# When a batch's weights and rows enter the DMA queue: ring weights by halves in six slots, rows of x behind a slot's swaps, the first output rows a slot sooner

## The chip, the core and the metric

The kernel runs on one core of a Trainium2 chip, in float32 throughout. The metric is the device time of one execution in microseconds, lower is better. TensorE (PE in the profile) multiplies, VectorE (DVE), ScalarE (ACT) and GpSimd (POOL) do the rest, and SyncE (SP) issues nearly all transfers, one after the other, in the order in which the program writes them down.

## The reference

Cross-attention of a sequence to a context that serves as keys and values, with a layernorm before and a residual after. There are 8 batches of 256 rows, 256 context rows and 1024 columns, 32 heads of 32.

```python
x = (hidden - mu) * rsqrt(var + 1e-5) * ln_gamma + ln_beta
Q = split_heads(x @ Wq.T)          # K = V = split_heads(ctx)
scores = einsum('bhsd,bhtd->bhst', Q, K) * 32 ** -0.5
probs  = softmax(where(mask, scores, -inf))
attn   = einsum('bhst,bhtd->bhsd', probs, V)
out    = hidden + attn.reshape(B, S, 1024) @ Wout.T
```

## The kernel before

**Slots.** The work of a batch is cut into 8 slots of 4 heads each, so there are 64 slots, numbered n = 8 b + i. The order of all instructions is written out by hand in one loop over n. In slot n, PE computes the scores of slot n + 1 (L494), the products of probabilities and values of slot n - 2 (L645), and pieces of the two projections (L216). DVE, ACT and POOL do the softmax of slot n + 1.

**Queries seven products at a time.** From batch 2 on, Q = xn Wq is made by a Strassen-like scheme of seven smaller products, one in a slot, the first in slot first = 8 (b - 1) + 2 (`firsts`, L817): S1, S4, A11, S2, S3, A22, A12. Each has 64 matmuls, 16 for each of four blocks of columns. Three of them take their weights from one buffer of 1 MB called `ring`: S1 uses T1, A11 (slot first + 2) uses B11, and S3 (slot first + 4) uses T3. T1, B11 and T3 are made once in the first batches and kept in DRAM (`kept`, L405 to L411). For batches 3 to 7 they are fetched into the ring each time by `load_ring(name, half)` (L417, L419), 512 KB a half; half 0 holds the first two blocks, so the first 32 matmuls of a product, half 1 the last 32. A half can only be overwritten when the product before has read it.

**Swaps.** The transposed probabilities of a slot go through four small transfers on SP: a first pair pT<-pT (L623), which waits for ACT's copies (`aside`, L564) and DVE's transposes (L558), and a second pair pT<-pc (L627), which overwrites what the first pair reads and so waits until it has landed. The end of `softmax_parts` writes down, in this order: the loads in the list `ahead`, the first pair, the loads in the list `between`, the second pair.

```python
for r in range(2):
    nc.sync.dma_start(pT[ts(2 * r, K), 1], pT[ts(2 * r + 1, K), 0])
for load in between:
    load()
for r in range(2):
    nc.sync.dma_start(pT[ts(2 * r + 1, K), 0], pc[ts(2 * r, K)])
```

In slots below 8 and above 55 this tail runs inside the next slot's softmax, while the `ahead` loads stay where they are.

**Other transfers.** Each slot loads keys (L135, 256 KB for two slots) or values (L143, 512 KB for two slots) in `between`. `load_x` (L129) brings the rows of a later batch for its layernorm, 512 KB for each half of the rows; DVE takes their statistics (L234) and transposes them (L323), then 16 moves of 64 KB each (`move_x`, L339) stand behind the swaps of slots first - 6 to first - 4 (4, 6 and 6 of them). `load_res` (L149) brings rows of x for the residual, 256 KB in four pieces a batch, to which POOL adds one product (L762) and DVE the others (L771) before they are stored (L772).

**Where the loads stand before the change.** T1's halves in `between` of slots first - 3 and first - 2; both halves of B11 in `ahead` of slot first; both halves of T3 in `ahead` of slot first + 2. Rows of x in `between` of slots first - 13 and first - 12 (first - 12 and first - 11 for batch 3). The first output rows in `between` of the batch's slot i = 0.

Of the kernel before, what the change touches and what calls it, by code (L numbers as in the profile page):

```python
# [59 lines left out]
def xattn_kernel(  # L60
# [11 lines left out]
    B, S, D = x.shape  # L72
# [3 lines left out]
    NQ = NC  # L76
# [9 lines left out]
    N = B * NQ  # L86
# [75 lines left out]
    B11, B21, B22, T1, T2, T3, T4 = range(7)  # L162
# [222 lines left out]
    SPLIT = 2  # L385
# [423 lines left out]
    for n in range(N):  # L809
# [7 lines left out]
    firsts = {NQ * (b - 1) + 2: b for b in range(SPLIT, B)}  # L817
# [1 line left out]
    assert not any(n in products and new_qs[n] for n in range(N))  # L819


    loads, stats, norms, trans, moves, biases, masks = (
        {n: [] for n in range(N)} for _ in range(7)
    )
    for b in range(1, B):
        first = NQ * (b - 1) + 2
        if b == 1:
            when = dict(moves=())
        elif b == 2:
            when = dict(  # L830
                loads=(0, 1), stats=(2, 3), norms=(3, 4), trans=(4, 5),
                moves=tuple(5 + (i + 2) // 6 for i in range(16)),
            )
        else:
            when = dict(
                loads=(first - 12, first - 11) if b == SPLIT + 1 else (first - 13, first - 12),
                stats=(first - 10, first - 8) if b == SPLIT + 1 else (first - 11, first - 9),
                norms=(first - 8, first - 7), trans=(first - 7, first - 6),
                moves=tuple(first - 6 + (i + 2) // 6 for i in range(16)),
            )  # L840
        for table, key in (
            (loads, "loads"), (stats, "stats"), (norms, "norms"), (trans, "trans"),
        ):
            for i, n in enumerate(when.get(key, ())):
                assert n < first
                table[n].append((b, i))
        for n in range(N):
            part = [i for i, slot in enumerate(when["moves"]) if slot == n]
            if part:
                assert n < first - 1  # L850
                moves[n].append((b, part))
        biases[NQ * b - 2].append(b)
        if b % 2 == 0:
            masks[NQ * b - 7].append(b)
# [18 lines left out]
    S3_SLOTS = [(b, NQ * b + {0: NQ, 1: NQ - 1}.get(b, NQ - 2)) for b in range(B)]  # L873


    away, rings = {n: [] for n in range(N)}, {n: [] for n in range(N)}
    for n, name, half in (
        (8, "T1", 0), (8, "T1", 1), (9, "B11", 0), (10, "B11", 1), (13, "T3", 0), (14, "T3", 1),
    ):
        away[n].append(partial(keep_wq, name, half))  # L880
    for n, b in firsts.items():
        for slots, name in (((n - 3, n - 2), "T1"), ((n, n), "B11"), ((n + 2, n + 2), "T3")):
            if b > SPLIT:
                for half, slot in enumerate(slots):
                    rings[slot].append(partial(load_ring, name, half))


    ln_stats(0, 0)
# [17 lines left out]
    for c in range(NC):  # L906
        copy_x0(1, c, nc.scalar if c < NC // 2 else nc.vector)
    first = softmax_parts(0, (partial(copy_q, 1), partial(copy_q, 2)), (), (), {}, [
        partial(ln_stats, 1, 0), partial(ln_stats, 1, 1),
        partial(ln_norm, 1, 0, nc.vector),  # L910
    ])
# [16 lines left out]
    for b in range(B - 1):  # L928
        done, ends = 0, b == B - 2
        for i, counts in enumerate(steps_of(b)):  # L930
            n = NQ * (b + 1) + i
# [15 lines left out]
    for n in range(N):  # L947
        b, i = divmod(n - NQ, NQ)
        new_q = new_qs[n]
        between = []  # L950
        if n % 2 and n + 1 < N:
            between.append(partial(load_v, n + 1))
        elif n % 2 == 0 and n + 4 < N:
            between.append(partial(load_k, n + 4))
        ahead = rings[n]
        if n + 3 in firsts or n + 2 in firsts:
            between, ahead = between + ahead, []
        if b >= 0:
            if b == B - 2 and i - 1 in (5, 6):
                between.append(partial(send, b, *ENDS_TO[i - 1]))  # L960
            if i < 4:
                between.append(partial(load_res, b, *((0, 0), (0, 1), (1, 1), (1, 0))[i]))
        between += [partial(load_x, *args) for args in loads[n]]
        between += [partial(load_mask, one) for one in masks[n]]
        if n in (2, 4):
            between.append(partial(load_wo, B21, n // 2 - 1))
# [205 lines left out]
```

## Time and profile before

| | us |
|---|---|
| median of 3 runs | 565.37 (564.01 to 566.51) |
| the profiled execution, whole | 565.4 |
| its span, first to last instruction | 563.6 |
| PE busy in the span | 556.2 |
| DVE, ACT, POOL busy | 467.4, 423.4, 394.8 |

PE's clock is granted in full through the whole span. The DMA engines move 119.43 MB, 212 GB/s on average. Times in the profile count from the span's start. A matmul's start is measured and its end is modelled. In the tables of waits a row names the waiting engine and line, what it waited for, and then the total, the number of times and the longest. "SPq" is SP's queue as it issues; the duration of an issue is not that of the transfer.

### The profile page before, as it was taken

The numbers are of one execution on the slowest core, as the hardware profiler recorded it, in microseconds if no ns is written. First come the engines' busy times: TensorE is split into PE (matmuls) and PEld (weight loads), VectorE is DVE, ScalarE is ACT, GpSimd is POOL, SyncE is SP. The second block draws the span as 40 slices with busy tenths as digits, with TensorE's granted clock in tenths as the row PEclk, the third lists the DMA queues.
The fourth block names the chain that finished last, engine by engine and source line by source line (L and its number), as shares of the span: only waits on it lengthen the run. The fifth ranks groups of instructions, "written<-read, shape, count | busy, mean of one in ns | idle before, by whom it ended". The sixth has DMA issues, their size and how long they took to land.

```text
span 563.6 us, 26534 instructions
## 1 busy us (share of the span) xinstructions
PE 556.2 (99%) x10364; PEld 350.8 (62%) x10364; DVE 467.4 (83%) x1716; ACT 423.4 (75%) x1464; POOL 394.8 (70%) x636
## 2 busy tenths in 40 slices
PE   8999999999999999999999999998999999999997
PEld 8666664666656667566765676566765767644443
DVE  5979889999997988888898888986878878879923
ACT  3699998898768867787777977777767776869920
POOL 2688887899786675876569665776658657448780
PEclk9999999999999999999999999999999999999999
DMA  8967657966798767887779668786667874536751
GB/s 302 396 187 208 168 158 213 305 199 168 226 299 248 217 181 197 259 249 222 196 223 283 204 185 232 237 263 174 166 168 251 260 207 135 153 101 184 208 170 74
DMA packets 47244, 119.43 MB, mean 212 GB/s; under 512 B 8976, under 2 KB 9744, under 8 KB 47120
## 3 DMA queue, kind: packets, MB, share of 16 engines
q1 hardware_dynamic: 46976, 117.74, 69.8%
q8 instruction: 82, 1.34, 1.0%
q14 instruction: 42, 0.34, 0.2%
q10 hardware_dynamic: 144, 0.01, 0.0%
HBM read 66.33 MB, written 11.53 MB: 138 GB/s over the span
## 4 chain that ended last, share of the span: by engine, by line
PE 77%; DVE 6%; POOL 6%; DMA 5%; SPq 2%; issue 2%; ACT 2%; DVEq 0%; POOLq 0%
PE po_S L216 17%; PE pq_A L216 16%; PE pv L645 10%; PE sc L494 9%; PE po_A L216 8%; PE pq L216 6%; PE pq_S L216 6%; PE po_end L216 3%; DVE pT L558 2%; DMA pT<-pT 2%; DMA r<-in_x_dram 2%; ACT e L537 1%; POOL e L552 1%; DVE e L533 1%; PE po_last L216 1%
## 5 line engine op out<-in xcount | busy, mean ns | idle before, releaser
L552 POOL TENSOR_SCALAR e<-e,rden 128x256 f32<-128x256 f32 x466 | 215.4, 479 | 119.8 <-DVE rden L544 116.9
L537 ACT ACTIVATE e<-e,mn 128x256 f32<-128x256 f32 x512 | 254.1, 502 | 41.7 <-DVE mn L533 41.3
L558 DVE STREAM_TRANSPOSE pT<-e 128x512 f32<-128x512 f32 x256 | 179.0, 704 | 35.6 <-POOL e L552 26.9
L533 DVE CUSTOM_DVE_ANT_0 e<-sc,mb 128x256 f32<-128x256 f32 x512 | 185.3, 416 | 22.0 <-PE sc L494 21.4
L564 ACT COPY pc<-pT 128x512 f32<-128x512 f32 x128 | 78.9, 617 | 54.7 <-DVE pT L558 35.2
L537 ACT ACTIVATION_READ_ACCUMULATOR e<-e,mn 128x1 f32 x512 | 98.2, 192 | 0.0
L645 PE MATMUL pv<-pT,v 64*32 64x128 f32 x4096 | 74.4, 274 | 0.4 <-DMA pT<-pc 0.4
L216 PE MATMUL po_S<-wo,at 128*64 128x512 f32 x304 | 73.9, 599 | 0.0
L645 PEld LDWEIGHTS pv<-pT,v 64*32 64x32 f32 x4096 | 57.0, 105 | 26.6 <-ACT pc L564 10.8
L494 PE MATMUL sc<-k,qa 32*64 32x256 f32 x2048 | 72.1, 387 | 0.2 <-ACT qa L301 0.2
L494 PEld LDWEIGHTS sc<-k,qa 32*64 32x64 f32 x2048 | 37.6, 131 | 49.2 <-issue 33.0
L216 PE MATMUL po_A<-wo,at 128*64 128x512 f32 x256 | 58.6, 599 | 0.0
L216 PE MATMUL pq<-xnT,wq 128*64 128x256 f32 (+3 forms) x544 | 58.4, 369 | 0.0
L216 PEld LDWEIGHTS pq_A<-xnT,wq 128*64 128x64 f32 x832 | 46.6, 137 | 7.1 <-issue 5.7
L216 PE MATMUL po_S<-wo,s 128*64 128x512 f32 x208 | 49.8, 600 | 0.7 <-DVE r L771 0.7
L216 PEld LDWEIGHTS pq<-xnT,wq 128*64 128x64 f32 x544 | 36.8, 136 | 19.1 <-issue 1.7
L216 PE MATMUL pq_A<-xnT,wq 128*64 128x128 f32 x832 | 47.8, 273 | 0.0
L544 DVE RECIPROCAL rden<-den 128x2 f32<-128x2 f32 x256 | 38.3, 150 | 7.3 <-ACT e L537 6.2
L533 DVE DVE_READ_ACCUMULATOR2_ANT mn<- 128x1 f32 x512 | 42.6, 83 | 0.0
L216 PEld LDWEIGHTS po_A<-wo,at 128*64 128x64 f32 x256 | 16.9, 136 | 30.0 <-issue 28.7
L762 POOL TENSOR_TENSOR r<-r,p 128x512 f32<-128x512 f32 x24 | 30.8, 1282 | 6.8 <-DMA r<-in_x_dram 4.4
L216 PEld LDWEIGHTS po_S<-wo,at 128*64 128x64 f32 x304 | 20.3, 136 | 21.9 <-issue 21.6
(100 smaller groups left out, 646.1 us busy)
## 6 DMA issues: line engine op xcount, KB each, us to landing
v<-in_kv_dram SPq DMA_DIRECT2D x32, 512.0 KB, 4.8
pT<-pT SPq DMA_DIRECT2D x128, 128.0 KB, 3.2
pT<-pc SPq DMA_DIRECT2D x128, 128.0 KB, 4.1
ring<-kept_T SPq DMA_DIRECT2D x20, 512.0 KB
k<-in_kv_dram SPq DMA_DIRECT2D x32, 256.0 KB, 3.8
x<-in_x_dram SPq DMA_DIRECT2D x15, 512.0 KB, 5.6
r<-in_x_dram SPq DMA_DIRECT2D x28, 256.0 KB, 4.5
out_dram<-r SPq DMA_DIRECT2D x28, 256.0 KB, 2.6
```

The costliest lines, as they stand in the source:

```text
L216: nc.tensor.matmul(out[ts(w, P // 2)], stationary[:, ts(w, P // 2)], moving, **flags)
L494: nc.tensor.matmul(scs[n][j][ts(w, P // 2), s, :], qa[r, n % NQ, ds(s * P + w * P // 2, P // 2)], ks[n - n % 2][r, n % 2, :], start=True, ...
L533: nc.vector.tensor_tensor_reduce(out=e[:, s, :], in0=pss[j][:, s, :], in1=mbs[n // NQ], scale=1.0, scalar=NO_SCORE, op0=ALU.add, op1=ALU.m ...
L537: nc.scalar.activation(e[:, s, :], e[:, s, :], AF.Exp, bias=mn[:, s : s + 1], scale=-1.0, accum_out=den[:, s : s + 1],)
L544: nc.vector.reciprocal(rden, dens[j])
L552: engine.tensor_scalar(es[j][:, s, :], es[j][:, s, :], rden[:, s : s + 1], 1.0, ALU.mult, ALU.mult,)
L558: nc.vector.transpose(pT[:, :, :, j, :, :].rearrange("p a i s k -> p (a i) s k"), es[j].rearrange("p s (b t) -> p b s t", t=K),)
L564: nc.scalar.copy(pc[:, :, ts(j, 2)], pT[:, 1, :, ts(j, 2)])
L645: nc.tensor.matmul(pvs[n][r][j * HD : (j + 1) * HD], vs[n - n % 2][ts(r, 2 * K), i, ds(n % 2 * P + j * HD, HD)], pT[ts(r, 2 * K), :, i, j, ...
L762: nc.gpsimd.tensor_tensor(r, r, p1s[b], ALU.add)
```

## The change

The ring halves no longer go out in pairs. For batches 3 to 7:

| load | before | after |
|---|---|---|
| T1, half 0 | `between` of slot first - 3 | `ahead` of slot first - 2 |
| T1, half 1 | `between` of slot first - 2 | `ahead` of slot first - 1 |
| B11, half 0 | `ahead` of slot first | `between` of slot first |
| B11, half 1 | `ahead` of slot first | `ahead` of slot first + 1 |
| T3, half 0 | `ahead` of slot first + 2 | `between` of slot first + 2 |
| T3, half 1 | `ahead` of slot first + 2 | `ahead` of slot first + 3 |

Rows of x for batches 3 to 7 move from `between` of a slot to `ahead` of the next, which is behind the second pair of swaps of the old slot and in front of the first pair of the new one. The first output rows of a batch (`load_res(b, 0, 0)`) go from slot i = 0 to `between` of slot i = 7 before it. The amount of data and all work of the engines stay the same.

```diff
             when = dict(
-                loads=(first - 12, first - 11) if b == SPLIT + 1 else (first - 13, first - 12),
+                early_loads=(first - 11, first - 10) if b == SPLIT + 1 else (first - 12, first - 11),
...
-        for slots, name in (((n - 3, n - 2), "T1"), ((n, n), "B11"), ((n + 2, n + 2), "T3")):
+        for slot, name in ((n - 2, "T1"), (n, "B11"), (n + 2, "T3")):
             if b > SPLIT:
-                for half, slot in enumerate(slots):
-                    rings[slot].append(partial(load_ring, name, half))
+                (rings if name == "T1" else rings_between)[slot].append(partial(load_ring, name, 0))
+                rings[slot + 1].append(partial(load_ring, name, 1))
...
-        ahead = rings[n]
-        if n + 3 in firsts or n + 2 in firsts:
-            between, ahead = between + ahead, []
+        ahead = [partial(load_x, *args) for args in early_loads[n]] + rings[n]
+        if i == NQ - 1 and b + 1 < B - 1:
+            between.append(partial(load_res, b + 1, 0, 0))
         if b >= 0:
             if b == B - 2 and i - 1 in (5, 6):
                 between.append(partial(send, b, *ENDS_TO[i - 1]))
-            if i < 4:
-                between.append(partial(load_res, b, *((0, 0), (0, 1), (1, 1), (1, 0))[i]))
-        between += [partial(load_x, *args) for args in loads[n]]
+            if 0 < i < 4:
+                between.append(partial(load_res, b, *((0, 1), (1, 1), (1, 0))[i - 1]))
+        between += rings_between[n] + [partial(load_x, *args) for args in loads[n]]
```

More of the change, by code (lines that the diff above doesn't have):

```diff
@@ L819, in xattn_kernel @@
     assert not any(n in products and new_qs[n] for n in range(N))
-    loads, stats, norms, trans, moves, biases, masks = (
-        {n: [] for n in range(N)} for _ in range(7)
+    loads, stats, norms, trans, moves, biases, masks, early_loads = (
+        {n: [] for n in range(N)} for _ in range(8)
     )
@@ L841, in xattn_kernel @@
         for table, key in (
-            (loads, "loads"), (stats, "stats"), (norms, "norms"), (trans, "trans"),
+            (loads, "loads"), (early_loads, "early_loads"), (stats, "stats"), (norms, "norms"), (trans, "trans"),
         ):
@@ L873, in xattn_kernel @@
     S3_SLOTS = [(b, NQ * b + {0: NQ, 1: NQ - 1}.get(b, NQ - 2)) for b in range(B)]
-    away, rings = {n: [] for n in range(N)}, {n: [] for n in range(N)}
+    away, rings, rings_between = ({n: [] for n in range(N)} for _ in range(3))
     for n, name, half in (
```

## The prediction

> **What bounds the kernel now.** I read the page's busy shares first, then the waits of TensorE, then those of the DMA queue, then the queue in order of time. The page:
>
> ```profile
> span 563.6 us, 26534 instructions
> ...
> PE 556.2 (99%) x10364; PEld 350.8 (62%) x10364; DVE 467.4 (83%) x1716; ACT 423.4 (75%) x1464; POOL 394.8 (70%) x636
> ...
> PE 77%; DVE 6%; POOL 6%; DMA 5%; SPq 2%; issue 2%; ACT 2%; DVEq 0%; POOLq 0%
> ```
>
> TensorE (PE) is busy for 556.2 of 563.6 us. The chain of waits runs through DVE, POOL and DMA for a fifth of the span, which looks like room; the waits say how much there is. First PE's own waits, then one of the queue's (total, times, longest):
>
> ```profile
> PE pq_S L216 <- issue: 1.7, 1, 1.7
> ...
> PE po_S L216 <- DVE r L771: 0.7, 1, 0.7
> PE pv L645 <- DMA pT<-pc: 0.4, 1, 0.4
> ```
>
> ```profile
> SPq L627 <- DMA pT<-pT: 63.3, 49, 5.5
> ```
>
> Inside the work PE lacks a result only twice, for 0.7 and 0.4 us; the 1.7 us of "issue" have no cause that the profile names. So a transfer that comes sooner can win about 1 us, at most about 3, while one that comes too late stops the engine that sets the end. The question is lateness. The queue itself waits 63.3 us at L627: the second pair of swaps (pT<-pc) overwrites what the first pair (pT<-pT, L623) reads, so SP stands still until the first pair has landed, and everything behind stands with it. Here is the queue through slots 23 and 24 (start, duration):
>
> ```profile
> 221.88 0.53 SPq L772 DMA_DIRECT2D out_dram<-r  x1
> 222.51 1.15 SPq L623 DMA_DIRECT2D pT<-pT  x2
> 223.71 0.57 SPq L143 DMA_DIRECT2D v<-in_kv_dram  x1
> 224.33 0.45 SPq L419 DMA_DIRECT2D ring<-kept_T  x1
> 224.87 1.15 SPq L627 DMA_DIRECT2D pT<-pc  x2
> 226.11 0.54 SPq L772 DMA_DIRECT2D out_dram<-r  x1
> 227.00 2.18 SPq L623 DMA_DIRECT2D pT<-pT  x2
> ...
> 229.85 0.45 SPq L419 DMA_DIRECT2D ring<-kept_T  x1
> 230.42 1.40 SPq L149 DMA_DIRECT2D r<-in_x_dram  x1
> 233.57 1.15 SPq L627 DMA_DIRECT2D pT<-pc  x2
> ```
>
> Two things are to be seen. From first to second pair takes 2.36 us (222.51 to 224.87) with no large load in front, and 6.57 us (227.00 to 233.57) behind v, a ring half, a pair of swaps and a store. And T1's second half goes out at 229.85, inside that wait; it doesn't stand behind it.
>
> **The change, part by part.** *T1, second half.* It moves from between the swaps of slot first-2 to the front of slot first-1. In the queue that is behind the second pair: past the 3.7 us wait just shown and the pair's own 1.15 us. S1, the first product of a batch, needs it for its second 32 of 64 matmuls. The chain in order of time gives S1 of batches 4 to 7, S3 of batch 4 and the stop of 1.7 us (start, us):
>
> ```profile
> 236.27 3.49 PE pq_S L216 x64
> ...
> 269.75 3.65 PE pq_A L216 x64
> ...
> 303.42 3.49 PE pq_S L216 x64
> ...
> 370.20 3.50 PE pq_S L216 x64
> ...
> 382.03 1.69 issue
> ...
> 438.99 3.49 PE pq_S L216 x64
> ```
>
> Batch 3's S1 stands in PE's timeline, where the 0.7 us wait follows it:
>
> ```profile
> 168.38 3.66 PE L216 MATMUL pq_S<-sx,ring 128*64 128x128 f32 x64
> 172.76 1.94 PE L216 MATMUL po_S<-wo,s 128*64 128x512 f32 x8 [0.72 <-DVE r L771]
> ```
>
> The second half is needed 1.75 us after S1 starts (half of 3.49). Issue today in batches 3, 5, 6 and 7 (batch 4's is 229.85 above):
>
> ```profile
> 164.24 0.44 SPq L419 DMA_DIRECT2D ring<-kept_T  x1
> ```
>
> ```profile
> 296.90 0.54 SPq L419 DMA_DIRECT2D ring<-kept_T  x1
> ```
>
> ```profile
> 362.74 0.45 SPq L419 DMA_DIRECT2D ring<-kept_T  x1
> ```
>
> ```profile
> 431.40 0.45 SPq L419 DMA_DIRECT2D ring<-kept_T  x1
> ```
>
> How long 512 KB takes to land, and how fast the DMA engines move data in a full stretch:
>
> ```profile
> v<-in_kv_dram SPq DMA_DIRECT2D x32, 512.0 KB, 4.8
> ...
> ring<-kept_B SPq DMA_DIRECT2D x10, 512.0 KB, 7.5
> ...
> kept_T<-ring SPq DMA_DIRECT2D x4, 512.0 KB, 3.3
> ```
>
> ```profile
> 290.00:300.00 10.00, 10.00 (x162) 5.14 (x156) 8.69 (x31) 7.26 (x26) 9.06 (x17) 1.00 0.98 297
> ```
>
> The page has no landing for ring<-kept_T. I take v's 4.8 us: same size, one load at a time; B11's 7.5 is for two halves back to back, the store's 3.3 is the short end. A load of 512 KB (524 kB) in front of a swap holds it for 524/297 = 1.8 us.
>
> Now slots 23 to 25 again with the change. Rows of x (second half, for batch 5) now stand in front of slot 23's swaps: first pair at 222.51 + 0.5 = 223.0, landed after 2.36 + 1.8, so second pair at 227.2 instead of 224.87. It takes 1.15, the store 0.6, T1's first half, now here, 0.5: first pair of slot 24 at 229.4 instead of 227.00. From there to the second pair: at least 2.36 + 1.8 = 4.2 us (only the ring half in front), at most today's 6.57; I take 5.0, nearer the low end because less is in flight by then. Second pair at 234.4, T1's second half 1.25 later at 235.6, which is 5.8 us later than today, landed at 240.4. It is needed at 236.27 + 1.75 = 238.0: PE stops for 2.4 us. With the short ends (4.2 and 3.3) the load lands at 238.1 and the stop is 0.1; with the long ones (6.57 and 7.5) 6.7.
>
> The same 5.8 + 4.8 = 10.6 us after today's issues: batch 5 lands at 307.5, needed 305.2, stop 2.3; batch 6 at 373.3, needed 371.9, stop 1.4; batch 3 at 174.8, needed 170.1, stop 4.7. Batch 7 has no x rows in front (no batch 8), so 0.5 + 1.8 falls away: 431.40 + 3.5 + 4.8 = 439.7, needed 440.7, no stop. Batch 3's stop covers the 0.7 us wait after its S1, which is on a load of output rows that now goes out a slot sooner: net 4.0. Sum over T1: 4.0 + 2.4 + 2.3 + 1.4 = 10.1 us.
>
> In a sentence of its own, a rule of the Trainium skill (DMA: Bandwidth & Descriptors, Anatomy of one DMA): its fit, made for transfers issued by GpSimd, is 2.0 us plus bytes over 436e3 per us, 3.2 us for a half; by it each stop would be 1.6 us shorter and the whole change about +4 us instead of the sum below. The trace's 4.8 us, on this queue, decides for me.
>
> *T3, second half.* It moves to the front of slot first+3. In between stand slot first+2's second pair and four moves of xn (L339). Batch 4, slot 28:
>
> ```profile
> 260.13 1.15 SPq L623 DMA_DIRECT2D pT<-pT  x2
> ...
> 263.76 1.14 SPq L627 DMA_DIRECT2D pT<-pc  x2
> 265.01 3.45 SPq L339 DMA_DIRECT2D xnT<-xe  x4
> ```
>
> Without T3's 1 MB in front, the second pair can go 2.36 us after 260.13, at 262.5; 1.2 and the moves' 3.5 put the half at 267.2, landed 272.0. S3 needs it at 269.75 + 1.8 = 271.6: 0.4 us. Batches 3 to 6 have such moves: 4 x 0.4 = 1.6 us, from 0 (landing in 3.3) to 4 x 3.1 (in 7.5).
>
> *B11* goes the same way (first half between the swaps of slot first, second in front of slot first+1), with no moves behind it and a whole slot before A11: nothing. *x rows* reach DVE's statistics later; DVE idles for them 4.3 us in three places today:
>
> ```profile
> DVE st L234 <- DMA x<-in_x_dram: 4.3, 3, 3.6
> ```
>
> Such a wait, up to 3.6 us once a batch, falls in slot 23's softmax, whose swaps are held by the queue anyway: 0; without that cover it would push the first pair back by its length. Slot 6 loses a load in front of its second pair, so the 0.4 us wait of pv goes. *The first output rows* cost one more 256 KB in slot first-3; the gain is booked in batch 3.
>
> Sum: 10.1 + 1.6 - 0.4 = +11.3 us on this execution's own 565.4 us, which is also the median of the runs (565.37): **577 us**. Forecast's own range 569 to 584.
>
> **The rivals.** *In time:* fronts are filled while SP would idle for ACT anyway, and the loads are out before the swaps are ready. For it: batch 7 by my own sum; with 2.36 us from pair to pair and 3.3 us to land, batch 4's half is there at 229.4 + 2.4 + 1.2 + 3.3 = 236.3, before 238.0. Against it: 6.57 us today. Then only 0.7 + 0.4 us go: 564.3 us. *In time, and the burst was the cause of the 1.7 us "issue" stop* (at 382.03, in batch 6's second product, soon after both B11 halves go out together): 562.6. Against it: no other batch shows such a stop. This is the rival on the faster side; it decides if T1's half lands before S1 + 1.75. *The queue falls behind for good:* in the slots with moves SP has little idle time; each pair now waits 1.8 us longer, in slots 22, 23 and 24, and if nothing is caught up between, slot 22's 1.8 + 0.5 adds to batches 3 to 6: 4 x 2.3 more, and B11's and T3's halves begin to miss by as much, some 1 us each in four batches: 577 + 9 + 4 = 590.
>
> **How the numbers follow.** Forecast 0.60, in time 0.17, faster 0.09, behind for good 0.14. Half a per cent is 2.8 us, about what a measurement of this kernel tells from no change. Faster by more: 0.08; within: 0.18 (in time, and a little of the forecast's low end); slower: 0.74. The range reaches from just below the in-time case to just short of the last one's 590: 564 to 588, which leaves about 0.1 on each side.
>
> **What would show it.** In the waits of the changed kernel, PE (or its weight loads) on pq_S waiting for DMA ring<-kept_T, four times, 1.4 to 5 us each, in batches 3 to 6 and not in 7; in the timeline T1's second half issued right behind the second pair, some 6 us later against S1 than today; SP's total at L627 up from 63.3 us; pv's and po_S's waits gone. I am wrong if S1 runs its 64 matmuls in 3.5 us everywhere: then the halves land in time and the time is that of the first two rivals. If PE also waits on A11 or S3 by more than 1 us, the queue is falling behind.

## The result and the profile after

The change makes the kernel slower by 6.9%: 607.23 us median (604.19 to 608.77, six runs) against 565.94 us (563.36 to 571.43, six runs) on the same chip, a ratio of 1.0693 with a 95% interval of 1.0642 to 1.0744. In time that is +41.3 us; the prediction said +11.3 on the execution's own time. The sign and the place were right, the size was not. Medians are of all runs, while the ratios leave out runs over 1.5% slower than the fastest of the same kernel; where the two differ, the ratio counts. The profiled execution of after took 608.51 us, with a span of 606.7 us against 563.6.

The page of after, with the lines that answer to those shown of before; PEclk is the granted clock in 40 slices.

```profile
span 606.7 us, 26539 instructions
...
PE 568.2 (94%) x10364; PEld 357.4 (59%) x10364; DVE 466.0 (77%) x1716; ACT 424.0 (70%) x1464; POOL 394.7 (65%) x636
...
PEclk9999999999998999889999799988999999999999
...
PE 54%; DMA 16%; POOL 11%; DVE 8%; ACT 5%; SPq 3%; issue 3%; DVEq 0%; POOLq 0%
```

Two things grew. PE stands still for 606.7 - 568.2 = 38.5 us of the span, before 563.6 - 556.2 = 7.4: **31.1 us of stops**. And PE is busy for 568.2 us with the same 10364 matmuls, before 556.2: **12.0 us in which the same work took longer**; the granted clock is below nine tenths in six of the 40 slices. Together they are the 43.1 us of the span. DVE, ACT and POOL have the busy time that they had.

The waits of PE, then the one of SP's queue that the prediction followed (total, times, longest):

```profile
PE pq_S L216 <- DMA ring<-kept_T: 20.2, 5, 6.1
PE pq_A L216 <- DMA ring<-kept_T: 3.7, 3, 1.8
PE pq_S L216 <- POOL e L552: 2.9, 1, 2.9
PE pq_S L216 <- ACT e L537: 2.8, 2, 2.0
PE pv L645 <- DMA pT<-pc: 1.9, 1, 1.9
PE pq_S L216 <- POOL sx L442: 1.7, 1, 1.7
```

```profile
SPq L627 <- DMA pT<-pT: 95.9, 58, 5.2
```

S1 waits for the ring for 20.2 us in five places. The 2.9 and 2.8 us put down to POOL e and ACT e are the same thing: they stand ahead of S1's first 32 matmuls, and by the trace's semaphore events T1's first half had just landed: at 174.61, 326.92 and 404.57 us, with S1 starting at 174.75, 327.05 and 404.71. With 0.2 us more ahead of batch 4's S1, T1 stops PE for 26.1 us.

PE's timeline of after around S1 of batches 4, 5 and 7 (start, duration, work, and in brackets the idle time before it and its releaser):

```profile
222.09 1.12 PE L494 MATMUL sc<-k,qa 32*64 32x256 f32 x32
...
240.08 6.23 PE L216 MATMUL po_A<-wo,at 128*64 128x512 f32 x28
246.24 1.12 PE L494 MATMUL sc<-k,qa 32*64 32x256 f32 x32
...
249.66 1.97 PE L216 MATMUL pq_S<-sx,ring 128*64 128x128 f32 x32 [0.20 <-ACT at L658]
256.36 3.68 PE L216 MATMUL pq_S<-sx,ring 128*64 128x128 f32 x32 [4.74 <-DMA ring<-kept_T]
259.82 2.70 PE L216 MATMUL po_S<-wo,s 128*64 128x512 f32 x8
...
327.05 1.97 PE L216 MATMUL pq_S<-sx,ring 128*64 128x128 f32 x32 [0.84 <-ACT e L537]
335.12 3.68 PE L216 MATMUL pq_S<-sx,ring 128*64 128x128 f32 x32 [6.10 <-DMA ring<-kept_T]
...
480.04 1.92 PE L216 MATMUL pq_S<-sx,ring 128*64 128x128 f32 x32
483.62 1.97 PE L216 MATMUL pq_S<-sx,ring 128*64 128x128 f32 x32 [1.67 <-DMA ring<-kept_T]
```

In batch 4 the second half of T1 comes 4.74 us after the first 32 matmuls have ended; the prediction had 2.4. In batch 5 it is 6.10. In each of them the second 32 matmuls then take 3.68 us, almost twice the 1.97 of the first 32; the eight matmuls of po_S behind them take 2.70 and 2.57 us instead of 1.9. Batch 7, with no rows of x in front, stops for 1.67 us and goes on at full speed.

The clock by stretches of 10 us (busy time of PE, PEld, DVE, ACT and POOL, then the granted clock, the DMA share and GB/s):

```profile
170.00:180.00 10.00, 3.85 (x98) 2.59 (x79) 5.00 (x17) 4.02 (x16) 5.52 (x11) 0.98 0.71 184
180.00:190.00 10.00, 8.63 (x138) 5.75 (x140) 1.46 (x9) 3.71 (x10) 0.00 (x0) 0.68 0.69 195
...
250.00:260.00 10.00, 5.26 (x64) 5.02 (x62) 4.31 (x15) 3.40 (x13) 5.14 (x10) 0.73 0.83 234
```

So PE can lose twice in a stop: it waits, and what follows runs at half clock for some microseconds. The trace's own records of the granted clock have half of it in five stretches around these stops, three of 6.83 us and two of 3.41 us, 27.3 us in all.

From the starts of the scores (L494) in both timelines each slot's length can be compared. Slots 18, 26, 34, 42 and 50, where S1 of batches 3 to 7 runs, are longer by 11.8, 7.9, 9.7, 8.8 and 1.9 us, 40.1 in all; slots 22, 30 and 46, where S3 needs T3, by 0.4, 2.0 and 1.9. Slot 10 loses 2.0 us (S1 of batch 2 waits 1.7 for POOL's sx). Slot 9 wins 0.85 and slot 43 wins 2.0, where the stops of 0.4 (pv) and 1.7 us ("issue") were. These sum to 43.5; the other slots together give 0.4 back.

The queue of after, from the slot before those that the prediction showed (SP's timeline, slots 22 to 25):

```profile
225.01 0.43 SPq L129 DMA_DIRECT2D x<-in_x_dram  x1
225.55 1.15 SPq L623 DMA_DIRECT2D pT<-pT  x2
...
229.87 1.55 SPq L627 DMA_DIRECT2D pT<-pc  x2
231.47 4.90 SPq L339 DMA_DIRECT2D xnT<-xe  x6
236.47 0.53 SPq L772 DMA_DIRECT2D out_dram<-r  x1
237.04 0.46 SPq L129 DMA_DIRECT2D x<-in_x_dram  x1
237.61 1.15 SPq L623 DMA_DIRECT2D pT<-pT  x2
...
241.92 1.15 SPq L627 DMA_DIRECT2D pT<-pc  x2
...
244.19 0.42 SPq L419 DMA_DIRECT2D ring<-kept_T  x1
244.70 1.16 SPq L623 DMA_DIRECT2D pT<-pT  x2
...
250.12 1.49 SPq L627 DMA_DIRECT2D pT<-pc  x2
251.95 0.33 SPq L419 DMA_DIRECT2D ring<-kept_T  x1
```

To lay this beside before, both are counted from the start of slot 23 on PE, which is the row at 222.09 above and this one of before:

```profile
208.91 1.12 PE L494 MATMUL sc<-k,qa 32*64 32x256 f32 x32
```

| us from the start of slot 23 | before | predicted | after |
|---|---|---|---|
| first pair, slot 23 | 13.60 | 14.1 | 15.52 |
| second pair, slot 23 | 15.96 | 18.3 | 19.83 |
| first pair, slot 24 | 18.09 | 20.5 | 22.61 |
| second pair, slot 24 | 24.66 | 25.5 | 28.03 |
| T1's second half issued | 20.94 | 26.7 | 29.86 |
| S1's second 32 matmuls can start | on time (29.1) | 31.5 | 34.27 |

Of the 3.2 us by which the issue missed the prediction, 1.4 were there at the first pair of slot 23: the first half of the rows of x, one slot earlier, had not been caught up. From second pair to first pair took 2.78 us instead of 2.2, from first to second 5.42 instead of 5.0, and the last step 1.83 instead of 1.25.

### The profile page after: what moved, and what is told of

It reads as the page before. It is cut to its first block, busy times and chain, and to the rows that moved or that the text cites. A ratio compares the mean times of both kernels' runs of the same rounds, so it can differ in the third digit from the quotient of the medians.

```text
span 606.7 us, 26539 instructions
## 1 busy us (share of the span) xinstructions
PE 568.2 (94%) x10364; PEld 357.4 (59%) x10364; DVE 466.0 (77%) x1716; ACT 424.0 (70%) x1464; POOL 394.7 (65%) x636
## 4 chain that ended last, share of the span: by engine, by line
PE 54%; DMA 16%; POOL 11%; DVE 8%; ACT 5%; SPq 3%; issue 3%; DVEq 0%; POOLq 0%
PE po_S L216 13%; PE pq_A L216 10%; DMA pT<-pT 7%; DMA ring<-kept_T 7%; PE sc L494 6%; PE pv L645 6%; PE pq_S L216 6%; PE pq L216 6%; POOL e L552 4%; ACT e L537 3%; PE po_A L216 3%; DVE pT L558 3%; PE po_end L216 3%; DVE e L533 2%; POOL wo L182 2%
## 5 line engine op out<-in xcount | busy, mean ns | idle before, releaser
L552 POOL TENSOR_SCALAR e<-e,rden 128x256 f32<-128x256 f32 x466 | 215.4, 479 | 169.4 <-DVE rden L544 164.5
L494 PE MATMUL sc<-k,qa 32*64 32x256 f32 x2048 | 72.2, 387 | 0.2 <-ACT qa L301 0.2
L494 PEld LDWEIGHTS sc<-k,qa 32*64 32x64 f32 x2048 | 37.8, 131 | 49.1 <-issue 34.7
L216 PE MATMUL pq_S<-sx,ring 128*64 128x128 f32 x384 | 31.6, 335 | 27.8 <-DMA ring<-kept_T 20.2
L216 PE MATMUL po_S<-wo,s 128*64 128x512 f32 x208 | 52.0, 624 | 0.0
L216 PEld LDWEIGHTS pq_S<-sx,ring 128*64 128x64 f32 x384 | 28.4, 172 | 34.0 <-DMA ring<-kept_T 21.6
L464 ACT ACTIVATE qa<-pq_S,qa 128x128 f32<-128x128 f32 x48 | 13.7, 367 | 34.8 <-PE pq_S L216 34.8
```

Of the source, the lines that this page charges most:

```text
L216: nc.tensor.matmul(out[ts(w, P // 2)], stationary[:, ts(w, P // 2)], moving, **flags)
L464: nc.scalar.activation(x_part(b, "P1")[:, o] if p == 2 else to[:, o], pqs[b][:, o, :].rearrange("p (a k) -> p a k", a=NA) if p == 2 else p ...
L494: nc.tensor.matmul(scs[n][j][ts(w, P // 2), s, :], qa[r, n % NQ, ds(s * P + w * P // 2, P // 2)], ks[n - n % 2][r, n % 2, :], start=True, ...
L552: engine.tensor_scalar(es[j][:, s, :], es[j][:, s, :], rden[:, s : s + 1], 1.0, ALU.mult, ALU.mult,)
```

## The experiments

The ratios are to the kernel before on the same chip.

**One edit back at a time.** First T1's halves alone (`e1_t1_back`: after, with T1 where it was):

```diff
+                if name == "T1":
+                    rings_between[n - 3].append(partial(load_ring, name, 0))
+                    rings_between[n - 2].append(partial(load_ring, name, 1))
+                    continue
```

> The changed kernel with T1's halves alone back between the swaps of slots first-3 and first-2; rows of x, B11, T3 and the output rows stay as changed. Theory A (T1's halves stand too late in the queue, and a PE that stops for them then runs slowly for some microseconds): slots 18, 26, 34, 42 and 50, which lost 11.8, 7.9, 9.7, 8.8 and 1.9 us, are back at 8.4 us (9.3 in slot 18 at most), so about 567 us, what is left being T3's 2 us twice and 1 us in slots 9 and 10. Rival B (rows of x in front hold the swaps, and PE would stop for the swaps or for x's sums anyway): T1 is not the cause, only the last of several late things; slots 18 to 42 keep at least half of their loss, 585 us or more.

583.46 us (581.69 to 584.75) against 568.38, ratio 1.0272 (1.0204 to 1.034). T1's stops are gone but for one of 1.2 us; 15 us stay. PE now waits for T3 (pq_A for the ring, 5.4 us in 3 waits) and for the products of probabilities and values (pv, 3.1 us for ACT e and 1.5 of issue). T1's place is not all of it.

Then the rows of x alone (`e2_x_back`: after, with the rows where they were, T1 stays late):

```diff
-                early_loads=(first - 11, first - 10) if b == SPLIT + 1 else (first - 12, first - 11),
+                loads=(first - 12, first - 11) if b == SPLIT + 1 else (first - 13, first - 12),
```

> The changed kernel with rows of x alone back between the swaps of a slot earlier; T1's halves stay late. Theory A in the form of the prediction (x in front of slot first-3's swaps makes up most of the delay): batches 3 to 6 then look like batch 7, which has no such rows and lost 1.9 us: 5 x 2 us + T3's 4, about 578 us. Rival C (T1's new place alone, behind the second pair of swaps, does it): stops of 4 us or more in S1 of batches 3 to 6 remain, 595 us or more.

592.85 us (584.14 to 593.6) against 568.38, ratio 1.0354 (1.0238 to 1.047), which is 20 us, with 14 to 27 open. It lies between the two theories' numbers. pq_S waits for the ring 16.2 us in 6 waits, the longest 4.4. In the profiled execution (593.57 us) S1's five slots lose 21.0 us and T3's 5.2; 4.9 more are lost in slot 9, where pv waits 2.4 us for a swap, before any load of T1. So T1's new place stops PE with no row of x in front of anything: the prediction's own sum, without its 2.3 us for the rows, gives 2.5 us of stops there.

Both back, by the two edits above together (`e3_both_back`; left of the change are the halves of B11 and T3 and the output rows):

> T1's halves and rows of x both back; what is left of the change is B11 and T3 by halves and the first output rows a slot sooner. Theory A: no stop is left in S1, T3's second half may still be late behind the moves of xn (2 us in two batches), and the 0.7 us wait for the output rows is gone: 563 to 568 us. If the halves of B11 and T3 cost by themselves: above 570 us.

570.49 us (566.99 to 571.33) against 568.38, ratio 1.0018 (0.9985 to 1.005): no difference. T3's second half still stops PE (pq_A for the ring, 5.8 us in 3 waits); the stops of 1.7, 0.7 and 0.4 us that went away give half of that back.

And the rows of x alone, on the kernel before (`e8_x_only`):

```diff
-                loads=(first - 12, first - 11) if b == SPLIT + 1 else (first - 13, first - 12),
+                early_loads=(first - 11, first - 10) if b == SPLIT + 1 else (first - 12, first - 11),
...
+        ahead = [partial(load_x, *args) for args in early_loads[n]] + ahead
```

> The kernel before with the rows of x alone in front of the swaps a slot later, all else as before. Theory Q: x holds the swaps in two slots of a batch, but T1 goes out inside the wait, and T3 and B11 are loaded long before they are needed, so only the moves and swaps themselves are later: 568 to 575 us, with no stop for the ring. If x in front is what costs most by itself (theory of the prediction, taken literally): 580 us or more.

585.99 us (582.95 to 587.05) against 567.72, ratio 1.0275 (1.0195 to 1.0354). By the ratio that is 16 us (11 to 20) with T1, B11 and T3 in their old places, above the theory's 568 to 575 us. T1's halves are held up there too: PE waits for the ring 5.4 us in 4 waits, the longest 2.1, which the theory had ruled out. The largest new wait is POOL's, for rows for the output that stood in the queue behind (waits of POOL, then one place in its timeline):

```profile
POOL r L762 <- DMA r<-in_x_dram: 24.2, 4, 7.6
```

```profile
177.06 1.26 POOL L762 TENSOR_TENSOR r<-r,p 128x512 f32<-128x512 f32 x1 [7.55 <-DMA r<-in_x_dram]
```

The softmax's next eight L552 start right behind it, at 178.31. DVE waits for L762 in turn (25.4 us in 6 waits) and PE for DVE.

**Which transfer suffers.** The same, with the first output rows a slot sooner as in after (`e12_x_and_rows`):

```diff
+        if i == NQ - 1 and b + 1 < B - 1:
+            between.append(partial(load_res, b + 1, 0, 0))
...
-            if i < 4:
-                between.append(partial(load_res, b, *((0, 0), (0, 1), (1, 1), (1, 0))[i]))
+            if 0 < i < 4:
+                between.append(partial(load_res, b, *((0, 1), (1, 1), (1, 0))[i - 1]))
```

> The kernel before with the rows of x in front of the swaps a slot later and the first output rows a slot sooner; the ring halves as before. Theory (x alone cost 18 us because the queue pushed the first output rows back, and POOL's L762, DVE's L771 and PE's po_S with them): with the rows a slot sooner POOL no longer waits for r (24.2 us in 4 waits with x alone), the stops in slots 18, 26, 34 and 42 shrink, 572 to 577 us. Rival (x in front pushes back the swaps and T1, whatever comes with the output rows): still 583 to 588 us, with waits of pq_S for the ring or of pv for pT<-pc.

581.71 us (579.36 to 585.91) against 569.81, ratio 1.0228 (1.016 to 1.0296). POOL's wait for the rows falls from 24.2 to 2.3 us, but the time is above the 572 to 577 that I had expected: PE now waits for the swaps (pv for pT<-pc 6.2 us in 3 waits, the longest 4.0). The rows of x make some transfer behind them late; which one depends on what stands there.

The rows of x as late, but between the pairs and not in front of them (`e10_x_between_later`, on the kernel before):

```diff
-                loads=(first - 12, first - 11) if b == SPLIT + 1 else (first - 13, first - 12),
+                loads=(first - 11, first - 10) if b == SPLIT + 1 else (first - 12, first - 11),
```

> The kernel before with the rows of x a slot later, but still between the two pairs of swaps instead of in front of them. Theory (it is the place in front of a pair that PE's operands wait for that costs; 18 us with x alone in front of the swaps): between the pairs SP would stand still anyway, so 565 to 570 us. Rival 1 (it is that the rows come later and meet T1's halves and the moves of xn): like x in front, 580 to 590 us. Rival 2 (both): about 575 us.

577.67 us (575.37 to 578.38) against 568.18, ratio 1.0162 (1.0112 to 1.0212), near the second rival's 575 us. Here no swap and no T1 is late. DVE is: it comes to the statistics before the rows have landed, waits in order (19.5 us in 7 waits, before 4.3 in 3), and the sum of a batch's queries (L470) behind it comes late to PE. DVE's timeline, then PE's:

```profile
225.36 1.28 DVE L234 BATCH_NORM_STATS2 st<-x 128x6 f32<-128x512 f32 x2 [3.16 <-DMA x<-in_x_dram]
```

```profile
233.87 7.92 PE L216 MATMUL po_A<-wo,at 128*64 128x512 f32 x28 [1.67 <-DVE qa L470]
```

T1 in front of the swaps, but a slot sooner (`e11_t1_front_sooner`, on after):

```diff
-        for slot, name in ((n - 2, "T1"), (n, "B11"), (n + 2, "T3")):
+        for slot, name in ((n - 3, "T1"), (n, "B11"), (n + 2, "T3")):
```

> The changed kernel with T1's halves still in front of the swaps, but a slot sooner (slots first - 3 and first - 2). Theory (T1's stops are lateness of its issue against the scores): S1's stops for the ring in batches 3 to 6 go, and about what T1 back between the pairs has is left, 583 to 588 us. Rival (a 512 KB load in front of a pair of swaps holds the pair, wherever it is, and PE then waits for the swaps): 595 us or more, with waits of pv for pT<-pc or pT<-pT in place of those of pq_S for the ring.

584.59 us (581.18 to 587.79) against 568.18, ratio 1.0278 (1.0226 to 1.0331), the same as with T1 between the pairs (1.0272). pq_S waits for the ring 1.5 us in all, so S1's stops were lateness. The place in front of a pair isn't free either: pv waits for pT<-pc 6.4 us in 4 waits, with T1 between the pairs (e1) 1.2 us in one. That is the rival's sign, though not its 595 us.

**Order in the queue, or bytes in flight.** T1's halves on ScalarE's queue (`e5_t1_on_act`, on after), and then the rows of x of batches 3 to 7 as well (`e16_both_on_act`, with both edits):

```diff
-        nc.sync.dma_start(ring[:, pair].rearrange("p o c q -> p o (c q)"), kept[name][:, pair])
+        queue = nc.scalar if name == "T1" else nc.sync
+        queue.dma_start(ring[:, pair].rearrange("p o c q -> p o (c q)"), kept[name][:, pair])
```

> The changed kernel with T1's halves issued by ScalarE's queue instead of SP's, at the same places in the program. Theory Q (SP's queue is the clock of slots first-5 to first: each load in front of a first pair of swaps makes it land later, the second pair waits for that, and T1 stands behind it): T1 no longer waits for the second pair, its second half goes out some 3 to 8 us sooner against S1, and the stops in slots 18 to 50 fall from 40 us to 10 at most; T3's stops may grow, as when T1 went back: about 580 to 590 us. Rival E (the DMA engines are full, so T1 would land late wherever it is issued): the stops stay, 600 us or more.

585.39 us (583.1 to 588.97) against 567.72, ratio 1.027 (1.0163 to 1.0377). Like T1 back: T1's waits go to 2.3 us, and what stays are waits of pv for pT<-pc, 8.5 us in 3, the longest 4.6.

```diff
-        nc.sync.dma_start(xs[b][:, s, cols], x[b, ts(s, P), cols])
+        queue = nc.scalar if b > 2 else nc.sync
+        queue.dma_start(xs[b][:, s, cols], x[b, ts(s, P), cols])
```

> The changed kernel with T1's halves and the rows of x of batches 3 to 7 issued on ScalarE's queue instead of SyncE's; the places in the program, the bytes and everything else as in the changed kernel. Theory (what costs is the order in SP's queue: a load in front of a pair of swaps, and the pairs in front of T1): S1's stops and the stops of pv for the swaps are gone, and about what both back in their places on SP has, 566 to 573 us. Rival 1 (the same bytes in flight beside the swaps slow them, whichever queue issues them): 578 us or more, with pv waiting for pT<-pc. Rival 2 (ScalarE, which now waits for free buffers in order, becomes late): 578 us or more, with waits for ACT.

571.35 us (565.91 to 578.96) against 566.54, ratio 1.0044 (0.9996 to 1.0092). With the same bytes, issued from the same places in the program, 41 us fall to 5 by the medians; by the ratio a difference isn't clear of none. On ScalarE's queue T1's second half goes out 6.4 to 8.5 us after the start of slot first - 1 on PE, in after 9.6 to 18.4 (the table under e15 has each batch). PE's waits for the ring there (lines are one further down by the edit):

```profile
PE pq_A L217 <- DMA ring<-kept_T: 4.0, 3, 2.1
...
PE pq_S L217 <- DMA ring<-kept_T: 1.2, 2, 0.7
```

What is left is mostly T3's, as with both back. The bytes are not what costs; the lateness that the order of SP's queue makes is.

**T1's two halves, and what is caught up.** T1's first half alone a slot sooner (`e13_first_half_sooner`, on after):

```diff
+                if name == "T1":
+                    rings[n - 3].append(partial(load_ring, name, 0))
+                    rings[n - 1].append(partial(load_ring, name, 1))
+                    continue
```

> The changed kernel with T1's first half alone a slot sooner (in front of the swaps of slot first - 3); the second half stays in front of slot first - 1. Theory A (S1 ends when the second half has landed, and the first half's lateness only splits the same stop in two): S1 starts on time and the stops for the ring move to its second 32 matmuls, 600 to 609 us. Theory B (each half's lateness costs by itself; the first one's waits, the ones put down to POOL e and ACT e among them, add up to some 10 us in the changed kernel): 590 to 597 us.

605.28 us (601.11 to 608.31) against 569.81, ratio 1.0625 (1.0563 to 1.0687), theory A's number. Batch 4's S1 in PE's timeline:

```profile
245.32 1.92 PE L216 MATMUL pq_S<-sx,ring 128*64 128x128 f32 x32
251.36 3.41 PE L216 MATMUL pq_S<-sx,ring 128*64 128x128 f32 x32 [4.12 <-DMA ring<-kept_T]
```

S1 no longer waits for its first half, runs its first 32 matmuls and waits for the second half all the same. Counted from the slot's start on PE, the second 32 begin at 10.5, 12.1, 11.2 and 6.7 us in batches 4 to 7, in after at 10.1, 12.1, 11.9 and 6.6; only in batch 3 are they clearly sooner, 12.3 against 15.0. So the stops ahead of S1 in after are in the main part of the same lateness, not a price of their own. The first half has a price where it now stands, in front of the swaps of slot first - 3: pv waits for pT<-pc 8.6 us in 4 waits, in after 1.9 us in one.

The first half of the rows of x back in its old place, the second still in front (`e15_one_x_back`, on after):

```diff
-                early_loads=(first - 11, first - 10) if b == SPLIT + 1 else (first - 12, first - 11),
+                loads=(first - 12,) if b == SPLIT + 1 else (first - 13,),
...
+        if b > SPLIT:
+            early_loads[first - 10 if b == SPLIT + 1 else first - 11].append((b, 1))
```

> The changed kernel with the first half of the rows of x back between the swaps of its old slot; the second half alone stands in front of a pair. Theory (the queue does not catch up what the first half's slot loses, so T1's second half is some 9 us later and not 5.8): T1's stops shrink by about 2 us in each of batches 3 to 6, and the slowed clock behind some of them goes: 590 to 598 us. Rival, as in the prediction (what that slot loses is caught up in the next): the stops stay, 603 to 609 us.

604.6 us (603.65 to 605.85) against 569.81, ratio 1.062 (1.0568 to 1.0672): the rival's number, not mine. When T1's second half goes out, in us from the start of slot first - 1 on PE (L419 in SP's timelines against L494 in PE's, in e16 ScalarE's queue and lines two further down; S1's second 32 matmuls need it landed by 13.1 in batch 4 of before):

| batch | 3 | 4 | 5 | 6 | 7 |
|---|---|---|---|---|---|
| before | 7.2 | 5.1 | 5.0 | 4.1 | 3.9 |
| T1 late, rows of x back (e2) | 15.5 | 10.6 | 8.9 | 11.0 | 10.3 |
| one half of the rows back (e15) | 17.3 | 13.2 | 12.3 | 12.5 | 8.1 |
| after | 18.4 | 14.0 | 14.6 | 15.4 | 9.6 |
| both on ScalarE's queue (e16) | 7.0 | 7.2 | 7.7 | 8.5 | 6.4 |

The mechanism is there: the half is issued 0.8 to 2.9 us sooner in batches 3 to 6, so what the first rows hold up isn't caught up in full. But it is the smaller part. T1's move alone makes the half 3.9 to 8.3 us later than before, the second half of the rows 1.5 to 3.4 us more. And the time hardly follows: S1's five slots lose 34.7 us instead of 40.1, T3's lose 2.3 more than in after, and the mean granted clock is no better (0.974 against 0.977).

**The clock, and how tight the rest is.** To keep PE from standing still, S1's first 32 matmuls are made three times in batches 3 to 6, with the same result in the end (`e4_keep_busy`, on after):

```diff
-        for o in range(NK):
+        again = (0, 1) * 2 if name == "S1" and SPLIT < b < B - 1 else ()
+        for o in (*again, *range(NK)):
```

> The changed kernel; in S1 of batches 3 to 6 PE computes the first 32 matmuls three times instead of once (the result of the last pass counts), 3.5 us of work that falls into the wait for T1's second half; nothing else is changed, the loads are as late as before. Theory A's second part (after a stop PE runs on a lower granted clock): the 32 matmuls behind the wait take 1.8 to 2.2 us instead of 3.5 to 3.7 and the eight after them 1.9 instead of 2.1 to 2.7, so about 2.5 us less in each of four batches, 597 us, and the granted clock of the slices is near 1. Rival D (the matmuls behind the wait are slow because the DMA writes the ring at that time): they stay slow, 607 us or a little more.

614.4 us: three runs took 614.1 to 615.38 and one 601.87, too far apart for a ratio. In the profiled execution (614.1 us) the mean granted clock is 0.988 instead of 0.977, so half of the slowed time went, while T3 came late more often (pq_A for the ring 9.1 us in 4 waits) and the filler itself takes 3.5 us in a slot. In the run of 601.87 us the clock was granted in full. Whether the filler wins time, and what the clock costs by itself, runs this far apart don't tell.

The trace does answer rival D. In batches 5 and 6, with stops of 2.53 and 1.25 us, the 32 matmuls behind the wait take 1.97 us and the eight after them 1.89, right after the same DMA has written the ring (after: 3.68 and 3.46, then 2.57 and 2.12). Batch 5:

```profile
339.51 1.97 PE L216 MATMUL pq_S<-sx,ring 128*64 128x128 f32 x32 [2.53 <-DMA ring<-kept_T]
341.31 1.89 PE L216 MATMUL po_S<-wo,s 128*64 128x512 f32 x8
```

So it is the clock that slows them, not the writing.

Then less work for PE: A22's 64 matmuls are left out in batches 3 to 7, so the queries lack that product (`e6_less_after` on after, `e7_less_before` with the same edit on before):

```diff
-        for o in range(NK):
+        for o in () if name == "A22" and b > SPLIT else range(NK):
```

> The changed kernel without the 64 matmuls of product A22 in batches 3 to 7 (left out of the computation; its copy stays). That takes 3.5 us from slot first+5, in which theory Q says the queue and not PE sets the time. Theory Q: PE then waits that much longer for T1, and little of 5 x 3.5 = 17.5 us is won: 600 to 606 us. Rival F (the stops come on top of PE's work, PE remains the bound elsewhere): the time falls by nearly all of it, to 592 us or less.

> The kernel before, with the same 64 matmuls of A22 left out in batches 3 to 7, to read the run on the changed kernel by. PE is busy nearly throughout, so by both theories most of the 17.5 us should show if the other engines keep up: 550 to 558 us; if the queue or the softmax engines are close behind PE in these slots, less is won: 560 us or more.

609.27 us (605.92 to 611.77) against 567.72 for after, ratio 1.0688 (1.0595 to 1.0782), and 568.96 (567.34 to 571.56) for before, ratio 1.0005 (0.9966 to 1.0044). Some 17.5 us of PE's work (5 times 3.5) less win nothing in either. That after doesn't move is therefore no proof that the queue sets its pace, which is what I had wanted from it. Page and PE's waits of before without A22:

```profile
PE 545.5 (96%) x10044; PEld 332.4 (59%) x10044; DVE 467.5 (83%) x1716; ACT 423.3 (75%) x1464; POOL 394.8 (70%) x636
```

```profile
PE po_S L216 <- DVE r L771: 14.1, 6, 2.6
```

Most of what PE saves, it waits for DVE in the next slots. The rest goes to the clock: PE's busy time falls by 10.7 us (556.2 to 545.5) and not by 17.5, and the granted clock is 0.985 to 0.991 in all ten runs, in those of before on the same chip 0.994 or more.

**What the other parts give.** The first output rows alone, by the last diff of e12 on the kernel before (`e9_rows_only`):

> The kernel before with the first output rows alone a slot sooner. Theory (the losses come from the ring halves and the rows of x that stand in front of swaps): the 256 KB stay in `between` and are one piece more in a slot that has no output rows yet, so nothing is lost, and the wait of po_S for DVE r (L771) in batch 3 goes: 564 to 567 us where the kernel before has 566. Rival (any load more in a slot ahead of a batch's first product pushes the second pair of swaps back and makes PE wait): 568 us or more, with waits of pv for pT<-pc in slots 8 b + 8.

565.81 us (562.9 to 569.91) against 568.18, ratio 0.9977 (0.9948 to 1.0007): nothing lost, and no gain that can be told from none.

With B11's halves apart as well (`e14_rows_b11`):

```diff
                 for half, slot in enumerate(slots):
+                    if name == "B11":
+                        (rings if half else rings_between)[slot + half].append(partial(load_ring, name, half))
+                        continue
                     rings[slot].append(partial(load_ring, name, half))
...
+        between += rings_between[n]
```

> The kernel before with the first output rows a slot sooner and B11's halves apart (first half between the swaps of slot first, second in front of slot first + 1); T1, T3 and x as before. Theory (these are the parts of the change that cost nothing): 562 to 567 us where the kernel before has 566 to 568, and no stop of PE for the ring in A11. Rival (B11's second half in front of slot first + 1 holds swaps that PE needs): 569 us or more, with waits of pv in slots first + 2.

565.88 us (561.01 to 572.14, 12 runs) against 569.81 (17 runs), ratio 0.9945 (0.9905 to 0.9984), a little faster. Page and PE's waits of its profiled execution:

```profile
span 561.1 us, 26538 instructions
```

```profile
PE pq_S L216 <- DMA ring<-kept_T: 1.4, 1, 1.4
```

A11 doesn't wait for B11, and the stops in slots 9 and 43 are gone; the 1.4 us are T1's in batch 3. So the change holds two parts that cost nothing and win some half a per cent, T3's halves, which with these two make no difference (e3), and two that cost 41 us.

## Why the prediction was wrong in size

**Right.** That lateness is the question; that T1's second half goes out behind the second pair and stops S1 in batches 3 to 6; that batch 7 is nearly spared (no stop predicted, 1.7 us measured); that T3's second half stops S3; that B11's halves cost nothing (no wait for ring<-kept_B in after); that the stops of 0.4 us (pv) and 0.7 us (po_S) go. SP's total at L627 rose as it should, from 63.3 to 95.9 us.

**The step that failed: the stop of T1's second half.** The prediction had it 5.8 us later than before and a stop of 2.4 us in batch 4, 10.1 us (net of the 0.7 us wait that it covers) over batches 3 to 6. The half went out 8.9 us later against slot 23, and T1 stopped PE for 26.1 us: 7.5, 4.9, 6.9, 5.0 and 1.7 in batches 3 to 7, where the prediction had 4.7, 2.4, 2.3, 1.4 and 0. Its landing, "4.8 us", was fair: the page of after has 5.1 us for ring<-kept_T. The failing part is the queue's delay:

- What moving T1 behind a pair costs by itself. The step added 3.5 us for it in batch 4 (5.8 less 2.3 for the rows of x); with the rows back (e2) it is 5.5 there and 3.9 to 8.3 over the batches, and S1's slots lost 21.0 us by that alone.
- What the rows of x add. The step counted one slot's 2.3 us and took it that slot 22 had caught up its own. 1.4 of the 3.2 us missing in batch 4 were there before slot 23 began. That was my rival "behind for good", whose sign ("if PE also waits on A11 or S3 by more than 1 us") came for S3, with up to 1.8 us. But e15 shows that this carry-over is no more than a small part: with one slot's rows in front the ratio is 1.062, with both 1.0693, and the intervals overlap.

**The term that was left out: what a stop does to the clock.** The prediction priced a stop at its length. PE's busy time rose by 12.0 us, since S1's second 32 matmuls and what follows ran at half clock. This is in the timelines above (3.68 us instead of 1.97, 2.70 instead of 1.9), and e4's trace shows the same matmuls at full speed after shorter stops.

The Trainium skill ("TensorE: Matmul & The Clock Gate", section "Part 1: The HAM clock gate (the "warmup" mystery)") states that the array's clock falls to half after at least one idle window of about 3.4 us and comes back after a busy one. The row of 180 to 190 us agrees in size: with a clock of 0.68, and 0.98 in the row ahead, (0.32 + 0.02) x 10 = 3.4 us are lost, which is 6.8 us at half clock, two such windows.

**Smaller ones.** T3 stopped S3 by 3.7 us in 3 waits (1.6 predicted). *x rows* "0" held for DVE's wait in after (5.9 us in all, before 4.3), but not by much: as late and between the pairs, DVE loses 19.5 (e10). S1 of batch 2 waits 1.7 us for POOL, and pv 1.9 for a swap ahead of batch 3's S1; neither was named. The 1.7 us "issue" stop went also where only the output rows move (e9) and where only x moves (e8), with B11's halves still going out together, so that burst alone was not its cause. What was, no run shows.

The prediction's 11.3 with these: 15.3 more for T1 (26.1 against 10.1 + 0.7), 12.0 for the clock, 2.1 for T3, 1.7 and 1.9 for the two stops not named, and 1.7 back from "issue" make 42.6 of the 43.1 us of the span.

**How far the cause is settled.** With T1 late alone 3.5% are lost (e2), with the rows of x in front alone 2.7% (e1, e8), with neither 0.2% (e3), with both 6.9%: the two add up, within e2's interval. Moving both to another queue, on which T1 goes out up to 11 us sooner, takes all but 5 us away (e16). That the cause is lateness made by the order of SP's queue is shown. Which transfer suffers from the rows of x differs from run to run (e8, e12, e10). How much of the 41 us the slowed clock makes by itself is only read from the traces, since the runs that were to take it away lie too far apart (e4).

## What to carry to other kernels

A queue that issues in order and waits inside itself has a time table of its own: before a load is moved, follow the queue slot by slot from a point where it still runs idle, with what the slot before has left over, and don't take a delay as caught up unless the trace shows idle time there. Price a stop of PE as its length plus what the clock takes afterwards, here two fifths more (12.0 us beside 31.1). A load that suits no place in a crowded queue may fit in another engine's queue, where its place cost 5 us at most instead of 41.

## What was not expected of the hardware

**Short stops halve the clock, but not each of them.** A stop of 1.67 us was followed by 28 matmuls of po_A in 7.92 us (e10, above), where after, at 240.08, takes 6.23 for the same 28; the clock granted there, in stretches of 10 us:

```profile
234.00:244.00 10.00, 10.00 (x126) 3.78 (x127) 9.18 (x36) 7.15 (x25) 8.62 (x13) 0.83 0.85 258
```

That is 1.7 us lost, 3.4 us at half clock. The stop of 1.67 us in batch 7 of after left the clock alone. The same section of the Trainium skill says that the window runs freely, so that where a stop lies in it may decide; but a stop of half a window was enough here, where the page asks for an idle one.

The records of the granted clock in the traces (17 of the 18 have them) bear this out. Each record but a run's last one lasts a whole number of steps of 3.41 us. Cut at these steps, without the first 20 us and the last 8, the traces have 1692 stretches at full clock. Where PE stood still for more than 2.05 us of a stretch, half clock followed all 38 times; with 1.6 to 2.05 us it followed 7 times of 31, with less once in 1623. The stop in e10 lies whole in one stretch, 1.67 us; that in batch 7 of after is parted by a step into 1.37 and 0.3. The ends of matmuls are modelled, so the 2 us are an estimate.

**PE at 99% was not the only bound.** With 17.5 us of its work taken away the kernel before keeps its time (e7): PE waits 14.1 us for DVE's additions (L771), and the clock that falls behind these waits takes some 7 us more. A busy share of 99% says that PE is hardly ever late, not that the others have room.
